# Two layers of a graph network on one core: moving layer 1's exponential and layer 1's transpose a few places down in a hand-written order

## The chip, the cores and the metric

The kernel runs on one core of one Trainium2 chip. The metric is the device time of one execution in microseconds (us), the median of several runs. A profile of one execution, taken by the hardware profiler, stands beside the times. Its engines are called PE (matrix multiplication; PEld is its weight load), ACT (activation and copies, "ScalarE"), DVE (vector work), POOL (general work) and SP (which issues the DMAs).

## The reference, cut to what matters

There are 16 graphs of 1024 nodes with 64 features, and an integer adjacency matrix for each (about 9 neighbours a node). Two layers follow each other:

```
layer 0:  q,k,v = x@Wq+bq, x@Wk+bk, x@Wv+bv            (8 heads of 64)
          s = leaky_relu(q.k/8 + edge_bias[adj], 0.2), masked where adj == 0
          x = layernorm(x + (softmax(s) @ v) @ Wp + bp)
layer 1:  hp = x@lin_w.T + lin_b ;  u = hp@W1.T ;  v = hp@W2.T
          e_ij = a . leaky_relu(u_i + v_j, 0.2), masked where adj == 0
          x = layernorm(x + elu(softmax(e) @ hp))
```

## The kernel before

Because the graphs are sparse, the kernel does not compute all pairs. For each image (graph) it first makes lists of neighbours (`prepare`, cut into 41 small pieces of mostly DVE work). Rows go in groups of 8 that share up to 120 neighbour slots; 16 groups make a tile of 128 rows, and 8 tiles make an image.

Work on one tile is a chain of stages that are spread over several steps of one loop. In step `g`, layer 0 works on tile `g` and on the tiles just before it, layer 1 on tile `u = g - 12` and those just before it. The stages that this text speaks of, with their lines:

- `gather`: PE multiplies the features with one-hot matrices `f` (L516, 26 matmuls for each half of a tile, `hs` 0 and 1) into a PSUM tile `pg`; ACT copies it to `xg` (L522). DVE makes `f` from the list of columns (`indicate`, L492).
- `turn`: PE transposes the slots `xg` (L535, two halves of 4 matmuls, `pt`), ACT copies each half to `xn` (L536). Layer 0's halves use the two PSUM buffers that `queries` used before (read by DVE as `qp`, L626), layer 1's use those of the two gathers before it.
- Layer 0: `queries` (PE `pq`, L621, DVE `qp`, L626); `score` (PE `s`, L642; DVE adds `rowc` into `sc`, L650, then L658, L659); `exps` (ACT, L668); `divide` (DVE L675, POOL L676); `turn_weights` (PE `pp`, L684, ACT copies to `w`, L686); `attend` (PE `z`, L694, which reads `w` and `xn`; ACT copies `zT`, L699); `heads` (PE `po`, L710, ACT L717).
- Layer 1: `own_rows` (ACT `rw`, L767, POOL `rq`, L769); `project` (PE `pz`, L777 and L783; ACT L789 and DVE L790 make `r`); `weigh` (PE `e`, L804; DVE takes the row maximum `m`, L806); `exps` (ACT `e`, L812); `turn_weights` (one PE transpose, L818, and one ACT copy `eT`, L820); `attend` (PE `pa`, L829, ACT copy `aT`, L834); `rows` and `residual` (PE `back`, L289 and L726, DVE `o`, L842 and L843, and `y`, L732).
- At the start of an image's layer 1, PE makes `pu` (L757) and DVE `u` (L759). The norm of each layer runs in small parts on ACT (L565, L573) and POOL (L568 to L579).

The scores `s`, the heads `po` and the projection `pz` share one pair of PSUM buffers, in this order. The PSUM tile of `weigh` (`e`), the one of layer 1's transpose, and `back` share one single buffer.

Nothing is scheduled by the compiler: `manual_schedule` keeps each engine's instructions in the order in which the loop writes them, and each engine takes its own in that order. `lists.place(g, k)` puts pieces of the list making, and parts of the norms, at five places of a step. How many pieces falls to a step is fixed by its place in the image, so steps at the same place of different images look alike. I name a step by the tile of layer 1 (0 to 7) that `weigh` works on in it, and count the time of a step from the first transpose of layer 0's weights (L684) to the next step's.

The order of one step, as far as it matters, is this:

```
rows, queries, residual, project(layer 1), place 1,
gather(layer 1, first half), layer 1's transpose, layer 0's turn, place 2,
indicate, gather(layer 1, second half), weigh, layer 1's exps,
layer 0's turn_weights, layer 1's turn, place 3, indicate, own_rows,
attend(layer 0), attend(layer 1), place 4
```

Of the kernel before, what the change touches and what calls it, by code (L numbers as in the profile page):

```python
# [33 lines left out]
def kernel(  # L34
# [401 lines left out]
    def finish(b):  # L436

        flags, dg, rows_s = late.pop(b)
        mask = dbl.tile([P, NT, SLOTS], BF16, tag="mask", bufs=3, name=f"mask_{b}")
        nc.vector.tensor_scalar(mask[:, :, 0 : 2 * CAP2], rows_s, code, NEG, ALU.not_equal, ALU.mult)  # L440
        yield
        dgf = sml.tile([P, NT], F32, tag="dgf", bufs=2, name=f"dgf_{b}")
        nc.vector.tensor_scalar(dgf, dg, 1.0, None, ALU.is_ge)
        own = sml.tile([P, NT, GR], F32, tag="own", bufs=2, name=f"own_{b}")
        nc.vector.tensor_tensor(
            own, dgf.unsqueeze(2).to_broadcast([P, NT, GR]), own_i.unsqueeze(1).to_broadcast([P, NT, GR]), ALU.mult
        )
        nc.vector.tensor_scalar(mask[:, :, 2 * CAP2 : SLOTS], own, 0.0, NEG, ALU.is_equal, ALU.mult)
        yield
        nc.vector.tensor_scalar(dgf, dg, 2.0, None, ALU.is_ge)  # L450
        nc.vector.tensor_reduce(flags[:, 18:19], dgf, XX, ALU.max)
        fl = sml.tile([P, 1], F32, tag="fl", bufs=2, name=f"fl_{b}")
        nc.vector.tensor_reduce(fl, flags, XX, ALU.max)
        nc.vector.tensor_scalar(fl, fl, 0.5, None, ALU.is_ge)
        nc.vector.tensor_tensor(bad, bad, fl, ALU.max)
        masks[b] = mask
# [417 lines left out]
    l0, l1 = {}, {}  # L874

    def at(layers, step, name, *args):
        b, t = divmod(step, NT)
        if b in layers:
            getattr(layers[b], name)(t, *args)
# [29 lines left out]
    with tc.manual_schedule(engines={getattr(mybir.EngineType, e) for e in order}):  # L909
        first = prepare(0)  # L910
        for _ in range(PIECES - 1):
            next(first)
        l0[0] = Layer0(0)
        for _ in lists.side.pop():
            pass
        l0[0].load(0)
        l0[0].load(1)
        l0[0].constants()
        for _ in first:
            pass  # L920
        l0[0].indicate(0)
        l0[0].own(0)
        for _ in finish(0):
            pass
        for g in range(NT * B + LAG + 7):
            u = g - LAG
            b, t = divmod(g, NT)
            if t == 0 and 0 < b < B:
                lists.side.insert(0, finish(b))
            lists.place(g, 0)  # L930
            at(l0, g - 2, "exps", 0, range(4))
            at(l0, g - 1, "score", lambda: at(l0, g - 2, "divide", 0))
            if (g - 1) // NT not in l0:
                at(l0, g - 2, "divide", 0)
            back = ps_z.tile([P, 3, D], F32, tag="e", name=f"back_{g}") if g > 3 else None
            at(l0, g - 2, "exps", 1, range(2))
            at(l0, g, "gather", 0)
            at(l0, g - 3, "heads")
            at(l0, g, "gather", 1)
            at(l0, g - 2, "exps", 1, range(2, 4))  # L940
            at(l1, u - 3, "rows", back)
            at(l0, g - 3, "rows", back)
            at(l0, g, "queries")
            if t == 6 and b - 2 in l1:
                lists.side.append(l1[b - 2].end())
            at(l1, u - 3, "residual")
            at(l0, g - 3, "residual")
            at(l0, g - 2, "divide", 1)
            at(l1, u - 1, "project")
            lists.place(g, 1)  # L950
            at(l1, u, "gather", 0)
            at(l1, u - 2, "turn_weights")
            at(l0, g - 1, "turn")
            lists.place(g, 2)
            at(l0, g + 1, "indicate")
            at(l0, g + 2, "load")
            at(l1, u, "gather", 1)
            at(l1, u - 1, "weigh")
            at(l1, u - 1, "exps")
            if t == 2 and b - 1 in l0:  # L960
                x1 = l0[b - 1].end()
            at(l0, g - 2, "turn_weights")
            at(l1, u - 1, "turn")
            lists.place(g, 3)
            at(l1, u + 1, "indicate")
            at(l1, u + 2, "load")
            at(l0, g + 1, "own")
            at(l1, u + 1, "own")
            at(l1, u, "own_rows")
            if t == NT - 1 and b + 1 < B:  # L970
                l0[b + 1].constants()
            at(l0, g - 2, "attend")
            at(l1, u - 2, "attend")
            lists.place(g, 4)
            if t == 2 and b - 1 in l0:
                l1[b - 1] = Layer1(b - 1, x1)
                del l0[b - 1]
                l1[b - 1].load(0)
            if t == 3 and b - 1 in l1:
                l1[b - 1].sums()  # L980
            if t == 4 and b + 1 < B:
                l0[b + 1] = Layer0(b + 1)
            if t == NT - AHEAD and b + 1 < B:
                l0[b + 1].load(0)
# [415 lines left out]
```

## Time and profile before

| what | value |
|---|---|
| median of 3 runs | 2485.44 us (2482.44 to 2485.81) |
| the profiled execution | 2491.47 us, its span 2489.6 us |
| PE busy | 2260.9 us, 91% |
| DVE busy | 1813.8 us, 73% |
| ACT busy | 1613.4 us, 65% |
| POOL busy | 1206.3 us, 48% |
| mean granted clock of PE | 0.969 |

The profile counts an engine as busy while one of its instructions runs. "Idle before, releaser" is the time that an engine stood still ahead of an instruction and what ended it. In the slices of the page PE is at 9 tenths or more from about 250 us to 2430 us: the steps with both layers run from 275 us to 2360 us, and in the last 110 us only layer 1 is left.

### The profile page before, as it was taken

The page shows a single profiled execution, that of the slowest core. Times are in us where ns is not written, and L with a number is a line of the kernel's source. Part 1 is how long each engine was busy: PE and PEld are TensorE (multiplying, and loading weights), DVE is VectorE, ACT ScalarE, POOL GpSimd, SP SyncE. Part 2 cuts the span into 40 slices and gives each one's busy share as a digit, 9 for nine tenths or more (in the row PEclk, how much of TensorE's full clock was granted, in tenths as well). Part 3 has the DMA queues.
Part 4 walks back from the last instruction along what each step waited for, and adds up shares of the span by engine and source line. Part 5 has one row for each costly group of instructions (what it writes and reads, how often), then busy time and mean ns, then how long its engine had stood idle before and what let it go on. Part 6 is the DMA issues. An engine that isn't in the chain of part 4 may idle for free. (4 is left out here: it accounts for less than half of the span.)

```text
span 2489.6 us, 107460 instructions
## 1 busy us (share of the span) xinstructions
PE 2260.9 (91%) x46658; PEld 1870.6 (75%) x46658; DVE 1813.8 (73%) x4591; ACT 1613.4 (65%) x5585; POOL 1206.3 (48%) x1570
## 2 busy tenths in 40 slices
PE   5577999999999999999999999999999999999995
PEld 3466878787787877778787777878777787888764
DVE  5688788687877868687787868778786877866432
ACT  2255666667676676766666676766766676677853
POOL 1133535545454554545455454545545454545552
PEclk8798999999999999999999999999999999999998
DMA  4422422423333242333324232332433233132111
GB/s 103 131 70 93 132 90 76 145 78 108 107 95 109 71 144 85 104 94 101 104 85 135 87 113 83 112 103 79 142 90 110 82 113 103 57 104 71 61 38 29
DMA packets 192691, 238.78 MB, mean 96 GB/s; under 512 B 91732, under 2 KB 157332, under 8 KB 192212
## 3 DMA queue, kind: packets, MB, share of 16 engines
q1 hardware_dynamic: 192212, 231.85, 30.1%
q8 instruction: 368, 6.03, 1.0%
q14 instruction: 111, 0.91, 0.1%
HBM read 226.58 MB, written 5.21 MB: 93 GB/s over the span
## 5 line engine op out<-in xcount | busy, mean ns | idle before, releaser
L516 PE MATMUL pg<-f,x 128*64 128x272 bf16 (+2 forms) x13312 | 811.7, 274 | 44.0 <-DVE f L492 29.0
L516 PEld LDWEIGHTS <-x 128*64 128x64 bf16 x13312 | 669.5, 110 | 154.0 <-issue 125.2
L676 POOL TENSOR_TENSOR ls<-ls,den 128x480 f32<-128x480 f32 x256 | 295.0, 1152 | 641.2 <-DVE den L675 640.1
L522 ACT COPY xg<-pg 128x448 f32<-128x448 f32 x512 | 268.0, 526 | 338.7 <-PE pg L516 338.1
L492 DVE TENSOR_SCALAR f<-cb,jrow 128x2176 bf16<-128x2176 bf16 x512 | 432.4, 885 | 15.0 <-DMA cb<-col_d 15.0
L668 ACT ACTIVATE ls<-ls,mx 128x120 f32<-128x120 f32 x1024 | 390.9, 385 | 0.0
L536 ACT COPY xn<-pt 120x512 f32<-120x512 f32 x512 | 277.9, 601 | 21.7 <-PE pt L535 21.6
L535 PE MATMUL pt<-ident,xg 128*120 128x128 f32 x2048 | 272.6, 275 | 19.6 <-DVE qp L626 17.2
L769 POOL TENSOR_TENSOR rq<-rw,in_q 128x960 bf16<-128x960 bf16 x128 | 229.9, 1796 | 114.8 <-ACT rw L767 114.8
L535 PEld LDWEIGHTS pt<-ident,xg 128*120 128x120 f32 x2048 | 230.7, 138 | 27.9 <-DVE qp L626 18.7
L650 DVE TENSOR_TENSOR sc<-s,rowc 128x480 f32<-128x480 f32 x256 | 156.0, 651 | 120.8 <-PE s L642 119.0
L694 PE MATMUL z<-w,xn 120*64 120x64 f32 x4096 | 173.2, 227 | 65.9 <-ACT w L686 65.8
L694 PEld LDWEIGHTS z<-w,xn 120*64 120x64 f32 x4096 | 146.6, 138 | 99.4 <-ACT w L686 93.9
L789 ACT ACTIVATE r<-pz 128x480 f32<-128x480 f32 x256 | 131.8, 567 | 123.1 <-PE pz L783 123.1
L790 DVE SCALAR_TENSOR_TENSOR r<-pz,r 128x480 f32<-128x480 f32 x256 | 155.6, 649 | 72.6 <-ACT r L789 72.3
L668 ACT ACTIVATION_READ_ACCUMULATOR ls<-ls,mx 128x1 f32 x1024 | 194.4, 190 | 0.0
L658 DVE SCALAR_TENSOR_TENSOR ls<-sc 128x480 f32<-128x480 f32 x256 | 181.3, 708 | 0.0
L659 DVE TENSOR_REDUCE mx<-ls 128x4 f32<-128x480 f32 x256 | 167.2, 653 | 8.8
L501 POOL COPY xg<-xT 128x64 f32<-128x64 f32 x256 | 104.0, 421 | 111.8 <-PE pt L535 111.8
L626 DVE TENSOR_TENSOR qp<-pq,qb 128x256 f32<-128x256 f32 x256 | 96.2, 417 | 76.8 <-PE pq L621 76.8
L642 PE MATMUL s<-xg,qp 64*64 64x120 f32 x4096 | 148.0, 286 | 4.1 <-DVE qp L626 3.4
L829 PE MATMUL pa<-eT,xn 120*64 120x8 f32 x4096 | 145.7, 202 | 4.8 <-ACT xn L536 3.9
(228 smaller groups left out, 4181.0 us busy)
## 6 DMA issues: line engine op xcount, KB each, us to landing
cb<-col_d SPq DMA_DIRECT2D x271, 544.0 KB
ad<-in_adj_dram SPq DMA_DIRECT2D x256, 256.0 KB
xs<-in_x_dram SPq DMA_DIRECT2D x32, 128.0 KB
rows_s<-slot_d SPq DMA_DIRECT2D x256, 14.0 KB
out_dram<-o SPq DMA_DIRECT2D x32, 128.0 KB
col_d<-col SPq DMA_DIRECT2D x128, 4.2 KB
dg<-in_adj_dram SPq DMA_DIRECT2D x32, 2.0 KB
slot_d<-slot SPq DMA_DIRECT2D x16, 28.0 KB
```

The source lines that it names most:

```text
L492: nc.vector.tensor_scalar(fj.rearrange("p s n q k -> p (s n q k)"), cb.rearrange("p s n q k -> p (s n q k)"), jrow[:, j : j + 1], None, AL ...
L516: nc.tensor.matmul(pg[sub(n), :, FIRST * a_ + lo : FIRST * a_ + to], self.t3[:, k, 4 * hs + 2 * a_ + j, :], f[j][:, 2 * hs + a_, n, :, lo:to],
L522: nc.scalar.copy(dst, pg)
L535: nc.tensor.transpose(pt[:, q, :], xg[:, 4 * m + q, :], ident)
L536: nc.scalar.copy(self.xn[t][:, ts(m, 4), :], pt)
L650: nc.vector.tensor_tensor(sc, both[n], self.rowc[:, n, ts_].unsqueeze(2).to_broadcast([P, 4, SLOTS]), ALU.add)
L658: nc.vector.scalar_tensor_tensor(ls, scs[n], SLOPE, scs[n], ALU.mult, ALU.max)
L659: nc.vector.tensor_reduce(self.mx[:, n, ts_], ls, XX, ALU.max, negate=True)
L668: nc.scalar.activation(ls[:, q, :], ls[:, q, :], AF.Exp, bias=neg[:, q : q + 1], accum_out=den[:, q : q + 1])
L676: nc.gpsimd.tensor_tensor(ls, ls, den.unsqueeze(2).to_broadcast([P, 4, SLOTS]), ALU.mult)
L694: nc.tensor.matmul(zz[sub(n), q, :], xn[:, q, sub(n)], w_[n][:, q // 2, sub(q % 2)], start=True, stop=True)
L769: nc.gpsimd.tensor_tensor(rq, rw.unsqueeze(1).to_broadcast([P, NQ, SLOTS]), in_q.unsqueeze(2).to_broadcast([P, NQ, SLOTS]), ALU.mult)
```

## The change

Two calls move in the loop's order. Layer 0's `turn` is written ahead of layer 1's `turn_weights` (one transpose, one copy). Layer 1's `exps` (one exponential with its sum on ACT) is written behind layer 0's `turn_weights` and layer 1's `turn`. No instruction is added, removed or changed in form.

```
             at(l1, u, "gather", 0)
+            at(l0, g - 1, "turn")
             at(l1, u - 2, "turn_weights")
-            at(l0, g - 1, "turn")
             lists.place(g, 2)
             at(l0, g + 1, "indicate")
             at(l0, g + 2, "load")
             at(l1, u, "gather", 1)
             at(l1, u - 1, "weigh")
-            at(l1, u - 1, "exps")
             if t == 2 and b - 1 in l0:
                 x1 = l0[b - 1].end()
             at(l0, g - 2, "turn_weights")
             at(l1, u - 1, "turn")
+            at(l1, u - 1, "exps")
             lists.place(g, 3)
```

On ACT the exponential L812 so comes behind the copies L686 and L536 of the same step, and the copy L820 behind the two copies L536 of layer 0. On PE the transpose L818 comes behind the eight of L535. The orders of DVE, POOL and SP (which issues all DMAs) stay as they were.

More of the change, by code (lines that the diff above doesn't have):

```diff
@@ L951 @@
             at(l1, u, "gather", 0)
+            at(l0, g - 1, "turn")
             at(l1, u - 2, "turn_weights")
-            at(l0, g - 1, "turn")
             lists.place(g, 2)
@@ L958 @@
             at(l1, u - 1, "weigh")
-            at(l1, u - 1, "exps")
             if t == 2 and b - 1 in l0:
@@ L963 @@
             at(l1, u - 1, "turn")
+            at(l1, u - 1, "exps")
             lists.place(g, 3)
```

## Prediction

> **What bounds the kernel now.** I read the page's engine shares first, then the waits, then the timeline of single steps.
>
> ```profile
> PE 2260.9 (91%) x46658; PEld 1870.6 (75%) x46658; DVE 1813.8 (73%) x4591; ACT 1613.4 (65%) x5585; POOL 1206.3 (48%) x1570
> ```
>
> PE sets the pace. So a gain must come out of PE's idle time, or out of PE's speed. Among the waits, these are the ones that the two moved calls touch (us in total, times, longest):
>
> ```profile
> ACT e L812 <- DVE m L806: 112.3, 100, 2.4
> ...
> PE z L694 <- ACT w L686: 65.8, 123, 1.5
> ...
> PE pt L818 <- DVE den L675: 19.5, 26, 1.2
> ...
> PE pg L516 <- ACT xg L522: 12.5, 11, 1.2
> ```
>
> The first two are one story. ACT stands at layer 1's exponential until DVE has the row maximum; behind it in ACT's queue are the copies `w` that PE's `z` needs. The timeline of a step of tile 3 shows it:
>
> ```profile
> 1205.62 1.04 PE L535 MATMUL pt<-ident,xg 128*120 128x128 f32 x8
> ...
> 1206.56 0.27 DVE L806 TENSOR_REDUCE m<-e 128x1 f32<-128x120 f32 x1
> ...
> 1206.87 0.36 ACT L812 ACTIVATE e<-e,m 128x120 f32<-128x120 f32 x1 [1.88 <-DVE m L806]
> ...
> 1207.22 1.06 ACT L686 COPY w<-pp 120x512 f32<-120x512 f32 x2
> ...
> 1207.85 0.33 PE L694 MATMUL z<-w,xn 120*64 120x64 f32 x2 [1.19 <-ACT w L686]
> ...
> 1208.34 1.09 PE L694 MATMUL z<-w,xn 120*64 120x64 f32 x29 [0.16 <-ACT w L686]
> ```
>
> `weigh` ended at 1204.77, but DVE had list work and `f` ahead of `m` and took it at 1206.56. PE was through with layer 1's turn at 1206.66 and stood 1.19 + 0.16 = 1.35 us. Step by step through the timeline this wait is the same in every image: 1.35 us at tile 3, 1.64 at tile 5, 1.35 at tile 6, 0.34 at tile 1, none at tiles 0, 2, 4, 7. Thirteen images have all of them: 13 x 4.68 = 61 us of the 65.8 (the rest is ahead of layer 1's first step).
>
> The stretches of the windows view show a second price (length, busy time of PE, PEld, DVE, ACT, POOL, then PE's granted clock):
>
> ```profile
> 1207.03:1210.44 3.41, 2.43 (x68) 2.27 (x72) 2.87 (x7) 3.38 (x12) 0.40 (x2) 1.00 0.51 159
> 1210.44:1213.86 3.42, 3.42 (x62) 3.00 (x61) 0.94 (x2) 2.59 (x14) 3.34 (x6) 0.50 0.85 259
> ...
> 1500.57:1503.98 3.41, 2.53 (x72) 2.38 (x76) 2.76 (x7) 3.38 (x12) 0.50 (x2) 1.00 0.45 141
> 1503.98:1507.40 3.42, 3.42 (x95) 3.31 (x88) 2.63 (x6) 3.02 (x15) 3.34 (x6) 1.00 1.00 277
> ```
>
> A 3.41 us stretch that holds most of the wait and the small matmuls `z` and `pa` is followed by one at half the clock; where the wait falls across two stretches (the lower pair), it is not. Between 330 and 2142 us the profile has 17 half-clock stretches, all directly behind one of these waits: 7 at tile 3, 9 at tile 6, 1 at tile 5. A step of tile 6 takes 20.53 us with one (1259.55 to 1280.08) and 19.17 without (1551.89 to 1571.06): 1.36 us each. At tile 3 it is 18.2 against 16.6 to 17.6: about 1.1.
>
> **The change, part by part.** No instruction is added; POOL, DVE, SP and the DMAs keep their order. What moves is one exponential (0.36 us, 0.45 with its sum's read) on ACT, one transpose (0.32) on PE, one copy (0.27) on ACT.
>
> *The exponential behind `w` and `xn`.* `w` can now start when its transposes are done, 0.6 us after the step's start; both copies (1.06) end by 1.7, and PE is at `z` at 1.96 (1206.66 less 1204.70). The z-wait goes in all steps. What is late next differs.
>
> Tile 3. The next thing that PE needs from DVE is `qp`, for layer 0's turn. DVE is held by its own list loads (`ab` waits for the DMA `ad`, up to 2.48 us at 1213.02), which PE does not move. In 10 of 13 images DVE is free for the scores 6.7 to 7.5 us into the step and `qp` is there 4.2 to 4.5 us later, by 12.0; PE, which asked at 13.4 in steps without a half clock, asks at 12.0 without its wait. These keep the 1.35. In three DVE is free only at 9.1 to 9.4, `qp` comes at 13.4, and nothing is kept. 10 x 1.35 = 13.5 us.
>
> Tiles 5 and 6. Here DVE has no idle time worth the name from 1237.24 to 1265.79, and the projection needs the score buffers, which DVE frees:
>
> ```profile
> 1251.24 1.21 DVE L650 TENSOR_TENSOR sc<-s,rowc 128x480 f32<-128x480 f32 x2
> ```
> ```profile
> 1252.90 0.99 PE L777 MATMUL pz<-xg,w2d 64*64 64x480 f32 x8
> ```
>
> PE comes to `pz` 1.64 us sooner, at 1251.26, and waits for `sc` until 1252.45: a new wait takes the old one's place. At tile 6 the same happens at `po`. What both tiles keep is what DVE can move: in images without half clock it waits only 0.04 us for `pu` and nothing for the scores there, and its scores come 0.36 us sooner. About 0.4 of 3.3 us: 13 x 0.4 = 5 us.
>
> The half clock. With the waits gone, the stretches with `z` and `pa` are full as they are at tiles 0, 4, 7, where none follows. 7 x 1.1 + 10 x 1.36 = 21 us.
>
> *Here a rule speaks against me.* The Trainium skill ("TensorE: Matmul & The Clock Gate", section "HAM oscillation — how this bites in real kernels") has the rule that PE gaps over about 3.4 us are the ones to avoid. By it waits of 1.2 to 1.6 us cost no clock, and these 21 us would not come. The rows above show the half clock behind waits of 1.35 us, so I keep them.
>
> *Layer 0's turn ahead of layer 1's transpose.* L818 waited for DVE to be through with `back` (L843): 1.21 us at tile 2, 0.32 at tile 6. The turn waits only for `qp`, which DVE ends 0.4 us before that, and the later transpose is then covered by 1.04 us of turn. At tile 2 this starts PE 0.8 us sooner, but layer 1's turn then stands for ACT's `xg` at 1333.36, where it already waited 0.20; ACT is held there by POOL's norm (L573 1.90 us idle). Nothing is kept. At tile 6 it falls into the DVE-bound stretch.
>
> It adds a wait too. `weigh` writes the buffer that the copy `eT` empties, and this copy now stands behind two of 0.6 us. In most steps `xn` ended 0.77 us ahead of `weigh`, enough. Not at tile 1, where ACT has norm parts ahead:
>
> ```profile
> 1312.55 0.27 ACT L820 COPY eT<-pt 120x128 f32<-120x128 f32 x1
> 1312.70 1.09 ACT L536 COPY xn<-pt 120x512 f32<-120x512 f32 x2
> 1312.87 0.62 PE L804 MATMUL e<-r,a_two 128*32 128x120 f32 x16
> ...
> ```
> ```profile
> 1325.67 1.59 PE L516 MATMUL pg<-f,x 128*64 128x272 bf16 x26 [1.18 <-ACT xg L522]
> ```
>
> `eT` will end near 1313.9 and hold PE's `weigh` (behind it `pp`, the turn, `z`) by 1.0 us. But PE arrives 1.18 us early at the gather of the next step, whose buffer ACT frees after POOL's norm, and tile 1's own z-wait (0.34) goes. 1.0 is less than 1.18 + 0.34 = 1.52: covered. If POOL were not late there, it would cost 14 x 1.0 = 14 us.
>
> The exponential itself has time: its reader L818 comes a step later. `rw`, `zT`, `aT` and layer 0's exponentials behind it start up to 0.3 us later in steps without a wait; ACT's 1.7 us idle before the next gather copy covers that.
>
> *The last 110 us.* Layer 1 alone: `pa` waits 0.33 to 0.39 us for `xn`, which no longer stands behind the exponential. 11 x 0.25 = 3 us.
>
> Sum: 13.5 + 5 + 21 + 3 = 42.5 us off the profiled 2491.47, which is 2449. The median of the runs stands 6.0 below the profiled one: 2443.
>
> **Rivals.** (1) All waits go and nothing takes their place: 61 + 4 (L818 at tile 6) + 21 + 3 = 89 us, 2396. For it: DVE is only 73% busy. Against: its gapless 28.5 us around tiles 5 and 6. (2) The half clock stays, because the new waits (1.0 us at tile 2's layer 1 turn, next to small matmuls; 1.2 at tile 5's `pz`) trip it as often: 42.5 - 21 = 21 us gained, 2464. By the skill's rule it would be much the same. (3) Slower: `eT` behind the copies. The place is `weigh` at tile 1, the price 14 x 1.0 us, with a half clock behind each 14 x 1.36 more, 33 us. It decides once ACT or POOL pass the delay on (POOL's `rq` needs `rw` by 1320.02 and gets it 1.9 us early) and the gains of tiles 3, 5 and 6 (18.5) are lost to DVE: 2485 + 33 less the old half clocks 21, about 2497. (4) DVE takes all of it, and `z`'s wait only changes its name: 2485.
>
> **How the numbers follow.** Forecast 0.60 (30 to 61 us gained), rival 1 0.10, rival 2 0.18, rival 3 0.07, rival 4 0.05. A measurement of this kernel tells about 0.2% (5 us) from no change. Faster 0.87, same 0.05, slower 0.08. The range takes the forecast from twice its kept DVE-side gain (2 x 18.5 + 21 + 3 = 61, 2424) to rival 2 with 6 us of tile 1's price (2470), leaving out rivals 1, 3 and 4: 2424 to 2470.
>
> **What would show it.** Right: `z` waiting for `w` near 5 us, ACT no longer idle for `m`; new waits of `pz` and `po` at tiles 5 and 6 for DVE, of `weigh` for `eT` at tile 1, a longer one at tile 2's turn; hardly any half-clock stretch from 330 to 2142 us. Wrong: half-clock stretches in other places, or waits at tile 3's turn for `qp` in most images.

## The result and the profile after

The change makes no difference that can be measured. The median after is 2491.21 us (20 runs, 2484.62 to 2498.64), that of the kernel before beside it 2487.56 us (20 runs, 2479.69 to 2500.03); the ratio is 1.0005, with a 95% interval from 0.9993 to 1.0016. The forecast of 2443 us was too low, and the result lies above its range (2424 to 2470 us). The profiled spans are 2489.7 us after and 2489.6 before.

The page's engine line of the kernel after shows PE as busy as before, and DVE 41 us busier, with not one instruction more:

```profile
PE 2264.4 (91%) x46658; PEld 1867.1 (75%) x46658; DVE 1854.9 (75%) x4591; ACT 1604.5 (64%) x5585; POOL 1229.3 (49%) x1570
```

The waits of the kernel after (us in total, times, longest) show that the edit did what it says. `z` waits 5.8 us for `w` instead of 65.8. In its place stands a larger wait of `po` for DVE's scores:

```profile
PE po L710 <- DVE sc L650: 45.6, 15, 4.7
...
PE pz L777 <- DVE sc L650: 13.9, 15, 1.0
...
PE e L804 <- ACT eT L820: 13.2, 15, 0.9
...
PE z L694 <- ACT w L686: 5.8, 17, 1.2
```

To find the place, take a step from the first transpose L684 to that of the next step, as the prediction did. Counted so, a step begins behind the `weigh` that names it, and the `weigh` and the transpose L818 of the next tile fall at its end: the waits that the prediction puts at tile 2 and at tile 1's `weigh` stand at the ends of the steps of tiles 1 and 0. Average the steps of images 1 to 12 for each tile of layer 1 (worked out from the timelines of both kernels, us):

| tile | 0 + 1 + 2 | 3 | 4 | 5 | 6 | 7 | one image |
|---|---|---|---|---|---|---|---|
| before | 54.77 | 17.75 | 18.36 | 18.36 | 19.99 | 16.96 | 146.2 |
| after | 54.90 | 15.66 | 18.38 | 17.68 | 22.76 | 16.80 | 146.2 |

Tile 3 gains 2.09 us, tile 5 gains 0.68, and tile 6 loses 2.77: everything that the first two brought. The timeline of one step of tile 6 in the kernel after (it runs from 1248.84 to 1272.20) shows how:

```profile
1251.40 0.27 DVE L806 TENSOR_REDUCE m<-e 128x1 f32<-128x120 f32 x1
...
1252.06 0.38 ACT L767 ACTIVATE rw<-mask,ones 128x120 bf16<-128x120 bf16 x1
...
1252.49 3.00 DVE L492 TENSOR_SCALAR f<-cb,jrow 128x2176 bf16<-128x2176 bf16 x2
1252.52 2.40 POOL L769 TENSOR_TENSOR rq<-rw,in_q 128x960 bf16<-128x960 bf16 x1 [0.77 <-ACT rw L767]
...
1258.73 1.21 DVE L650 TENSOR_TENSOR sc<-s,rowc 128x480 f32<-128x480 f32 x2
...
1259.44 2.54 PE L710 MATMUL po<-zT,wvp 64*64 64x128 f32 x32 [2.98 <-DVE sc L650]
```

And the same place in the kernel before (its step runs from 1259.55 to 1280.08):

```profile
1262.51 1.47 DVE L492 TENSOR_SCALAR f<-cb,jrow 128x2176 bf16<-128x2176 bf16 x2
...
1264.48 1.79 POOL L769 TENSOR_TENSOR rq<-rw,in_q 128x960 bf16<-128x960 bf16 x1 [2.67 <-ACT rw L767]
...
1267.08 0.69 DVE L759 TENSOR_TENSOR u<-pu,rows_b 128x512 f32<-128x512 f32 x1 [1.29 <-PE pu L757]
```

Before, POOL's `rq` waited for ACT's `rw`, which stood behind the copies that stood behind the exponential. When `rq` began at last, 4.93 us into the step, DVE was done with both halves of `f`. After, ACT is not held: `rw` starts 3.22 us into the step instead of 4.42, `rq` 3.68 instead of 4.93, and so `rq` begins 0.03 us behind the first of the two `f`. The second `f` takes 2.31 us instead of 0.78 and ends 0.58 us after `rq`; `rq` takes 2.40 instead of 1.79 (medians over images 1 to 12, for both kernels). In images 0 and 9 `rq` comes 0.03 us ahead of both `f`: there `rq` keeps its 1.79 us and the first `f` takes 2.40. DVE has no idle time here, so the scores come 1.53 us later than they need, and PE stands 2.98 us at `po` (2.98 to 3.00 in eleven images, 3.42 in images 0 and 9).

This is not all of the 41 us by which DVE is busier. Summed over its instructions, `f` (L492) takes 24.5 us more and the list load L335 takes 26.6 more; in the run with the early `f` at tile 6 below, which is faster, L335 takes as much more (27.0) and `f` only 4.3.

A half clock follows. The windows view around the wait (length, busy time of PE, PEld, DVE, ACT, POOL, then PE's granted clock):

```profile
1255.10:1258.50 3.40, 1.35 (x26) 1.04 (x22) 3.30 (x11) 0.73 (x3) 1.39 (x2) 1.00 0.59 128
1258.50:1261.90 3.40, 2.46 (x32) 1.86 (x32) 3.37 (x7) 0.00 (x0) 1.40 (x2) 0.50 0.90 288
```

It does so in all 13 images. Between 300 and 2300 us both kernels run 58.0 us at half the clock: before at tiles 3, 6 and 5, after at tile 6 alone.

### The profile page after: what moved, and what is told of

It is laid out like the page before. It is cut to its first block, busy times and chain, and to the rows that moved or that the text cites. A ratio compares the mean times of both kernels' runs of the same rounds, so it can differ in the third digit from the quotient of the medians.

```text
span 2489.7 us, 107346 instructions
## 1 busy us (share of the span) xinstructions
PE 2264.4 (91%) x46658; PEld 1867.1 (75%) x46658; DVE 1854.9 (75%) x4591; ACT 1604.5 (64%) x5585; POOL 1229.3 (49%) x1570
## 5 line engine op out<-in xcount | busy, mean ns | idle before, releaser
L516 PE MATMUL pg<-f,x 128*64 128x272 bf16 (+2 forms) x13312 | 820.9, 276 | 38.5 <-DVE f L492 28.3
L492 DVE TENSOR_SCALAR f<-cb,jrow 128x2176 bf16<-128x2176 bf16 x512 | 457.2, 933 | 11.1 <-DMA cb<-col_d 11.1
L535 PE MATMUL pt<-ident,xg 128*120 128x128 f32 x2048 | 278.0, 278 | 33.6 <-DVE qp L626 21.5
L536 ACT COPY xn<-pt 120x512 f32<-120x512 f32 x512 | 277.1, 597 | 31.0 <-PE pt L535 27.6
L535 PEld LDWEIGHTS pt<-ident,xg 128*120 128x120 f32 x2048 | 225.5, 138 | 65.5 <-DVE qp L626 32.5
L769 POOL TENSOR_TENSOR rq<-rw,in_q 128x960 bf16<-128x960 bf16 x128 | 236.9, 1851 | 69.7 <-ACT rw L767 69.5
L686 ACT COPY w<-pp 120x512 f32<-120x512 f32 x256 | 138.1, 589 | 62.1 <-PE pp L684 62.1
L694 PE MATMUL z<-w,xn 120*64 120x64 f32 x4096 | 152.6, 227 | 5.8 <-ACT w L686 5.8
L501 POOL COPY xg<-xT 128x64 f32<-128x64 f32 x256 | 111.5, 453 | 91.3 <-PE pt L535 91.2
L777 PE MATMUL pz<-xg,w2d 64*64 64x480 f32 x1024 | 143.5, 573 | 14.4 <-DVE sc L650 13.9
L694 PEld LDWEIGHTS z<-w,xn 120*64 120x64 f32 x4096 | 133.4, 139 | 28.2 <-ACT w L686 27.5
```

Of the source, the lines that this page charges most:

```text
L492: nc.vector.tensor_scalar(fj.rearrange("p s n q k -> p (s n q k)"), cb.rearrange("p s n q k -> p (s n q k)"), jrow[:, j : j + 1], None, AL ...
L516: nc.tensor.matmul(pg[sub(n), :, FIRST * a_ + lo : FIRST * a_ + to], self.t3[:, k, 4 * hs + 2 * a_ + j, :], f[j][:, 2 * hs + a_, n, :, lo:to],
L535: nc.tensor.transpose(pt[:, q, :], xg[:, 4 * m + q, :], ident)
L536: nc.scalar.copy(self.xn[t][:, ts(m, 4), :], pt)
L694: nc.tensor.matmul(zz[sub(n), q, :], xn[:, q, sub(n)], w_[n][:, q // 2, sub(q % 2)], start=True, stop=True)
L769: nc.gpsimd.tensor_tensor(rq, rw.unsqueeze(1).to_broadcast([P, NQ, SLOTS]), in_q.unsqueeze(2).to_broadcast([P, NQ, SLOTS]), ALU.mult)
```

## The experiments

The first two take the two moves apart; the next three keep both and take the collision away in three ways; then the collision alone is put into the kernel before; the last three ask what the second move is worth without the collision, and whether the DVE-bound stretch can be shortened.

**The exponential alone.** The kernel before with only this:

```
-            at(l1, u - 1, "exps")
...
             at(l1, u - 1, "turn")
+            at(l1, u - 1, "exps")
```

> Only the exponential is moved; layer 1's transpose stays ahead of layer 0's turn. Theory 1 (collision: with the z-wait gone ACT makes rw 1.2 us sooner at tile 6, POOL's rq then runs beside DVE's second f of layer 1 (L492 2.31 us instead of 0.78), DVE hands over the scores late, PE waits 2.98 us at po and half a clock follows): tile 6 takes 22.5 us as in the changed kernel, the time is within 5 us of it, about 2490. Theory 2 (the stretch of tiles 5 and 6 is bound by DVE anyway, and any wait of PE at po trips the half clock): the same. Theory 3 (the second move eats the gain, because eT holds weigh 0.93 us at the end of tile 0's step and layer 1's turn then waits 0.98 us at tile 2): without it the steps of tiles 0 to 2 lose 2 us an image, 13 x 2 = 26 us, about 2465.

Measured: 2497.27 us, ratio 1.0026 [1.0008, 1.0044]. This is 5 us more than expected. About half of tile 3's gain is there (16.63), tile 6 takes 21.48 (22.5 was expected; PE waits 2.29 us at `po`), and its second `f` takes 2.32 us. So the collision comes with the exponential. The move of the transpose is not what eats the gain: without it the kernel is no faster. What the second move does for tiles 3 and 5 is seen in one wait, 0.67 us at each of them in all 13 images, which the full change does not have:

```profile
PE pt L818 <- DVE den L675: 33.2, 40, 1.2
```

**The turn alone.** The kernel before with only this:

```
+            at(l0, g - 1, "turn")
             at(l1, u - 2, "turn_weights")
-            at(l0, g - 1, "turn")
```

> Only layer 0's turn is moved ahead of layer 1's transpose. Theories 1 and 2: rw comes when it came before, so tile 6 stays at 20.5 us with or 19.2 without a half clock; eT's wait at weigh is covered by the gather's wait in the next step; 2487 within 5 us. Theory 3: slower by 13 x 0.9 = 12 us or more, about 2500.

Measured: 2490.3 us, ratio 0.9998 [0.9976, 1.002]: nothing in the total. Tiles 0, 1 and 2 take 17.41, 16.46 and 21.14 us, 55.0 together against 54.77. PE waits 0.92 us for `eT` at the end of tile 0's step, and that is given back in the next. But within the image the steps shift, which the expectation did not foresee: tile 3 takes 16.58 us instead of 17.75 and tile 6 18.76 instead of 19.99, while tile 5 takes 19.62 instead of 18.36. The half clock has gone to tile 5, where 10 of 13 images now have one (1 at tile 3, 3 at tile 6; 68.3 us in all against 58.0). Why it moves is not shown.

**`rq` later.** The kernel after with layer 1's `own_rows` (that is, `rw` and `rq`) behind both `attend` calls:

```
-            at(l1, u, "own_rows")
...
             at(l1, u - 2, "attend")
+            at(l1, u, "own_rows")
```

> The changed kernel with layer 1's own_rows behind both attends, so that ACT makes rw after zT and aT and POOL's rq starts near 4.9 us into the step of tile 6, when DVE's second f is nearly done (on POOL the order stays). Theory 1: that f takes 0.8 us again, the scores come 1.4 us sooner, the wait at po falls from 2.98 to 1.5 us or less, the half clock behind it goes, and tile 6 takes 18 to 19.5 us: 13 x 3.5 = 45 us less, about 2445. Theory 2: the wait of 1.5 us at po still trips the half clock, tile 6 takes 21 us: 13 x 1.4 = 18 us less, about 2472. Theory 3: no difference, 2490.

Measured: 2463.3 us, ratio 0.9881 [0.9849, 0.9912], between theories 1 and 2. The second `f` at tile 6 is back at 0.78 us and the step at 19.34 in the median (20.0 in the mean, since five of the 13 still have a half clock). What it costs elsewhere is a longer last stretch, in which layer 1 runs alone and needs `rq` soon: 142.2 us from the last transpose L684 to the end of the span, against 133.6 in the kernel after; PE's waits of `pz` for `rq` there are 9.0 us instead of 2.6.

**`f` earlier, in every step.** The kernel after with layer 1's `indicate` ahead of place 3:

```
+            at(l1, u + 1, "indicate")
             lists.place(g, 3)
-            at(l1, u + 1, "indicate")
```

> The changed kernel with DVE's f of layer 1 (indicate) ahead of place 3's list pieces, so that f is done before rq starts at tile 6; ACT's and POOL's orders stay. Theory 1: f takes 0.8 us, tile 6 takes 18 to 19.5 us, about 2445 if the list pieces do not meet rq in f's place. Theory 2: about 2472, half clocks stay. Theory 3: no difference, 2490.

Measured: 2465.05 us, ratio 0.989 [0.9861, 0.9919], between theories 1 and 2 as well. Tile 6 takes 19.47 us, with one half clock in the run. But at tile 3 the early `f` now stands ahead of DVE work that PE needs sooner: PE waits for the scores ahead of `pz` in 12 of 13 images (10.4 us, 0.6 in the kernel after), and the step takes 16.54 us instead of 15.66.

**`f` earlier, at tile 6 alone.** The same move under a condition:

```
+            if t == 3:
+                at(l1, u + 1, "indicate")
             lists.place(g, 3)
-            at(l1, u + 1, "indicate")
+            if t != 3:
+                at(l1, u + 1, "indicate")
```

> The changed kernel with layer 1's f ahead of place 3's list pieces in the steps of tile 6 alone. Theory 1 (the collision at tile 6 is what ate the gain): tile 6 takes 19.4 us, every other step and the end stay as in the changed kernel (tile 3 15.7, tile 5 17.7), so 13 x (22.8 - 19.4) = 44 us less than the changed kernel: about 2447. If what the earlier run gained came from f's place in the other steps: 2480 or more.

Measured: 2450.04 us, ratio 0.9846 [0.9821, 0.9871], 39 us below the kernel before beside it (2489.25). Two instructions moved by one place in one step of eight bring a gain near the forecast's (42.5 us). Its timeline, in a step of tile 6 from 1088.04 to 1107.37:

```profile
1090.79 1.47 DVE L492 TENSOR_SCALAR f<-cb,jrow 128x2176 bf16<-128x2176 bf16 x2
...
1091.71 2.19 POOL L769 TENSOR_TENSOR rq<-rw,in_q 128x960 bf16<-128x960 bf16 x1 [0.77 <-ACT rw L767]
...
1096.40 1.21 DVE L650 TENSOR_TENSOR sc<-s,rowc 128x480 f32<-128x480 f32 x2
...
1097.10 1.66 PE L710 MATMUL po<-zT,wvp 64*64 64x128 f32 x32 [1.45 <-DVE sc L650]
```

Now `f` is first and `rq` pays (2.19 instead of 1.79), which nobody waits for. PE waits 1.45 us at `po` instead of 2.98: the difference is the 1.53 us by which the second `f` was longer. The step takes 19.33 us in the median against 22.47; the other 1.6 us go with the half clock, which now comes in one of 13 images. Tile 3 keeps 15.76 and tile 5 17.67.

**The collision in the kernel before.** Layer 1's `indicate` moved behind place 4 at tile 6, so that it meets the late `rq`; neither move of the change:

```
             lists.place(g, 3)
-            at(l1, u + 1, "indicate")
+            if t != 3:
+                at(l1, u + 1, "indicate")
...
             lists.place(g, 4)
+            if t == 3:
+                at(l1, u + 1, "indicate")
```

> The kernel before (neither call moved), with layer 1's f behind place 4's list pieces in the steps of tile 6 alone, 1.9 us later, so that it meets POOL's rq (which starts 4.93 us into the step). No work is added. Theory 1: the f that starts beside rq takes about 2.3 us instead of 0.78, the scores come 1.5 us later, PE waits for them at po: tile 6 takes 21.5 to 23 us instead of 20.0, 13 x 1.5 to 3 = 20 to 39 us slower than before, about 2515. If DVE and POOL beside each other cost nothing: 2490 as before.

Measured: 2498.57 us, ratio 1.004 [1.0023, 1.0057]. Slower, but by about a third of what was expected. The collision itself is the same, in the timeline:

```profile
1264.29 3.01 DVE L492 TENSOR_SCALAR f<-cb,jrow 128x2176 bf16<-128x2176 bf16 x2
...
1264.45 2.27 POOL L769 TENSOR_TENSOR rq<-rw,in_q 128x960 bf16<-128x960 bf16 x1 [2.67 <-ACT rw L767]
...
1267.23 0.68 DVE L759 TENSOR_TENSOR u<-pu,rows_b 128x512 f32<-128x512 f32 x1
```

But `u` comes at 1267.23 in a step that begins at 1259.87, 7.36 us into it, as in the kernel before (7.53), where DVE stood 1.29 us idle for `pu`. The collision fills that idle time, and tile 6 takes 20.18 us on average against 19.99. So the price of 1.5 us is paid only where PE no longer arrives late, that is, where the exponential has been moved. Where the rest of the 9 us comes from is not settled: no one tile holds it.

**Fewer list pieces at tiles 5 and 6.** The kernel with the early `f` at tile 6, and another quota of list pieces for each step (two pieces moved from the steps of tiles 5 and 6 to those of tiles 7 and 0):

```
-    QUOTA = (3, 3, 5, 6, 6, 6, 6, 6)
+    QUOTA = (3, 3, 5, 6, 5, 5, 7, 7)
```

> As the run with f early at tile 6 alone, and two of the list pieces (0.95 us of DVE each) moved from the steps of tiles 5 and 6 to those of tiles 7 and 0. If what is left there is DVE's time, as forecast (pz waits 1.03 us at tile 5, po 0.79 at tile 6): both waits shrink to near nothing, 13 x 1.5 = 20 us less, about 2428. If PE's waits there have another cause: no difference, about 2447.

Measured: 2427.6 us, ratio 0.9748 [0.9721, 0.9776]. This is the fastest version of the study, and beats both kernels. Tile 5 takes 16.77 us and tile 6 18.42; tiles 7 and 0 pay 0.17 together. Between 300 and 2300 us there is no half clock at all. The waits left of the kernel after's 45.6 and 13.9:

```profile
PE po L710 <- DVE sc L650: 13.6, 16, 4.7
...
PE pz L777 <- DVE sc L650: 1.2, 4, 0.4
```

**The early `f` without the second move.** The kernel of the first experiment (the exponential alone) with `indicate` early at tile 6, by the same edit as above.

> This is the kernel with the moved exponential and layer 1's indicate ahead of place 3 where t is 3 (tile 6), but without the second move: layer 0's turn stays behind layer 1's transpose. Theory 1 (the second move has a use of its own once the collision of f and rq at tile 6 is gone: it takes layer 1's transpose of the weights away from its wait of 0.67 us for DVE at tiles 3 and 5): tiles 3 and 5 take 16.6 and 18.4 us instead of 15.8 and 17.7, so 13 x (0.87 + 0.71) = 20.5 us more than the kernel with both moves and the early indicate: 2470 us. Theory 2 (the second move changes the order of waits and nothing else, as it did alone): as fast as with both moves, 2450 us.

Measured: 2461.48 us, ratio 0.9888 [0.9869, 0.9907], 11 us slower than with both moves. Neither theory holds: tile 3 (16.58 against 15.76) and tile 5 (18.38 against 17.67) lose what theory 1 said, but tile 6 takes 18.64 instead of 19.47 and gives one of the two back. Tiles 5 and 6 together take 37.02 us in the one and 37.14 in the other: DVE sets the end of the pair, and a wait at tile 5 is only taken from the one at tile 6. What is left is tile 3: 13 x 0.82 = 10.7 us.

**The quota alone.** The kernel before with that quota and nothing else.

> The kernel before with the other quota of list pieces (3, 3, 5, 6, 5, 5, 7, 7: two pieces less at the steps of tiles 5 and 6, two more at those of tiles 7 and 0) and neither move. Theory 1 (the quota pays only where PE waits for DVE's scores at tiles 5 and 6, and in the kernel before PE stands there for the copy of the weights instead): the waits of z for w at tiles 5 and 6 (1.64 and 1.35 us) become shorter by less than half, because layer 0's f stays ahead of the row maximum in DVE's queue: 2475 to 2490 us. Theory 2 (fewer pieces are worth the same 22 us with or without the moves): 2466 us.

Measured: 2487.04 us, ratio 0.9993 [0.9975, 1.0012]: nothing in the total, as theory 1 said. In its waits `z` still stands for `w`:

```profile
PE z L694 <- ACT w L686: 62.0, 137, 1.5
```

At tile 5 that wait is what it was (21.4 us in all). At tile 6 it falls from 16.5 to 5.4 us, by more than half, against theory 1; but 8.1 us of it arise at tile 7, which had none. The steps shift with it: tile 6 takes 18.37 us instead of 19.99, tile 5 19.06 instead of 18.36 and tile 7 17.83 instead of 16.96, and of the half clocks seven are at tile 5, two at tile 3 and none at tile 6.

Fewer pieces on DVE are worth 22 us where PE waits for DVE's scores, and nothing in the kernel before. There PE still waits for a copy that ACT has queued behind the exponential; with the half clock moving as well, the runs do not part what each of the two takes.

## Why the prediction was wrong

By the tile table times 13 images, and the stretch behind the last full step:

| | forecast gain, us | measured gain, us |
|---|---|---|
| tile 3 (wait and half clock) | 13.5 + 7 x 1.1 = 21.2 | 27.2 |
| tiles 5 and 6 (wait and half clock) | 5 + 10 x 1.36 = 18.6 | -27.2 |
| tiles 0, 1, 2, 4, 7 | 0 | 0 |
| last stretch | 3 | -3.5 |

*The step that failed* is one clause at the head of the second part: "No instruction is added; POOL, DVE, SP and the DMAs keep their order." It is true, and it was used as if it said that their instructions keep their durations and their places against each other. The prediction followed `w`, `xn`, `rw` and `zT` on ACT, and asked of `rw` only whether it would be late ("start up to 0.3 us later in steps without a wait"). In the steps with a wait `rw` starts 1.2 us sooner, so does `rq`, and on POOL nothing holds it. The prediction did not ask what DVE would be doing then. The scores at tile 6, forecast to come "0.36 us sooner", come behind a second `f` that is 1.53 us longer.

Rows that should have warned stand in the profile of before. In its step of tile 6, the second `f` of layer 0 already runs beside another POOL instruction and takes 1.69 us instead of 0.78; 41 of the 512 `f` do so in that profile, each beside L468:

```profile
1259.10 2.39 DVE L492 TENSOR_SCALAR f<-cb,jrow 128x2176 bf16<-128x2176 bf16 x2
...
1259.21 1.70 POOL L468 TENSOR_TENSOR less_x<-less_x,x 128x512 f32<-128x512 f32 x1
```

And in the step of tile 5 `rq` already meets one of DVE's list instructions, which takes 0.19 us in its other places:

```profile
1244.35 0.19 DVE L376 TENSOR_TENSOR left<-left,left 128x32 int32<-128x32 int32 x1
...
1246.52 1.83 POOL L769 TENSOR_TENSOR rq<-rw,in_q 128x960 bf16<-128x960 bf16 x1 [2.89 <-ACT rw L767]
...
1246.73 1.66 DVE L376 TENSOR_TENSOR left<-left,left 128x32 int32<-128x32 int32 x1
```

The prediction called DVE gapless from 1237.24 to 1265.79 and read the 1.66 us as work. (After, `rq` meets another instruction of the same list piece at tile 5, L378, which takes 1.74 us: the same price, so nothing was lost at tile 5, and PE's new wait at `pz` is 1.03 us where 1.19 was forecast.)

*Half clock, 21 us.* Failed by the same step. The 58.0 us at half clock moved to tile 6 and stayed 58.0; with the collision gone 3.4 are left, and with the new quota none. The rule of the Trainium skill that was weighed against this term ("TensorE: Matmul & The Clock Gate", section "HAM oscillation — how this bites in real kernels") warns of PE gaps over some 3.4 us, and the prediction read it as saying that shorter gaps cost no clock. The waits of 2.98 to 3.42 us at `po` were followed by a half clock in 13 images of 13, so the runs stand against that reading here; but waits of 1.45 us at the same place were followed by one in a single image of 13 with the early `f`, and in five of 13 with `rq` later. So the length of the wait alone does not decide, nor does the time that PE is busy in a stretch of 3.41 us: in the kernel before, the stretches ahead of a half clock had PE busy for 2.07 to 2.49 us, and the stretch from 1824.84 us, with 1.77 us and a wait of 1.48 us in it, was followed by the full clock. What decides is open.

*Tile 3, 13.5 us.* Too small, and that it came this near is in part luck, since about half of the gain is the second move's (below). The forecast let three images of 13 wait for `qp` instead; none does, and the step takes 15.1 to 16.0 us in all.

*Tiles 5 and 6, DVE-bound.* Right as a limit. The forecast for the pair was 38.35 less (18.6 / 13) = 36.9 us; with the collision gone it takes 37.14.

*Layer 0's turn.* Right for tiles 0 to 2: `weigh` waits 0.93 us for `eT` (forecast 1.0) and the next gather's wait covers it; tiles 0, 1 and 2 change by 0.13 us together. Wrong in that it was put at nothing elsewhere. Once the exponential has moved, L818 would wait 0.67 us for DVE at tiles 3 and 5, and the second move takes that away: it makes 0.97 of tile 3's 2.09 us (15.66 against 16.63 with the exponential alone), which the prediction put down to the exponential.

*The last stretch, 3 us.* Wrong in sign. PE's waits at `pa` fall from 4.3 to 3.1 us, but those of `pz` for `rq` (L783) rise from 1.8 to 2.6, and the stretch has two pieces of half clock more, 3.4 us each.

*The rivals.* The result lies between rival 4 (2485 us) and rival 3 (2497) in its number. It is nearest to rival 4 in that nothing is gained and a wait for DVE takes the place of `z`'s, and to rival 2 in that the half clock stays, but none names the mechanism. Rival 4 had DVE take the gain by the work it has; what took it was work that grew.

## What to carry to other kernels

When an instruction is moved on one engine, list every engine that it releases sooner as well as those that it delays, and ask for each what will then run at the same time. Look in the trace for an instruction that takes several times its usual duration and see which engine was busy beside it: such a pair has a price that an unchanged order does not protect. An engine without idle time passes such a price on in full; one that waits anyway hides it.

## What the runs showed of the hardware

Some instructions of DVE and POOL shut each other out for the length of an instruction. A bf16 `f` of 0.78 us that starts while `rq` runs takes 2.31 us and ends 0.58 us after `rq`, whether it started 0.2, 0.5 or 0.7 us into it (37 cases in the kernel after, the run with the exponential alone and the collision in the kernel before). With `rq` only 0.03 us ahead it takes 2.40 and ends 0.58 us after `rq` too. The other way round, an `f` that comes first keeps its 0.78 us and `rq` grows from 1.79 to between 1.93 and 2.40. L376, which has two inputs, takes 1.66 us beside `rq` instead of 0.19. But the list instructions L390 and L392 (128x280) take 0.43 to 0.45 us within `rq`, as they do elsewhere (0.42 to 0.46).

The Trainium skill ("SBUF — State Buffer", section "Who interferes with whom") has this: VectorE and GpSimd share one pair of ports to SBUF, which tensor_scalar can take in its two-port modes and through which an operation with two SBUF inputs reads its second, and whoever issues first holds it for the whole instruction. The durations given here agree with it. That this port is the cause, and not another thing that the two engines share, no run here separates.
